# A graph transformer on one core: the last tile's query asked for earlier, and the order of two layer norms in eight blocks

## The chip, the cores and the metric

The kernel runs on one core of a Trainium2 chip. A core has five engines, each with its own queue of instructions that it works through in order: TensorE (PE in the profile; its weight loads are PEld) for matrix products and transposes, VectorE (DVE), ScalarE (ACT), GpSimd (POOL) and SyncE (SP), which only issues transfers. Engines wait for each other by semaphores. The metric is the device time of a whole execution in microseconds, of which 1.7 us lie outside the span from the first to the last instruction in the profiled execution.

## The reference, cut to what matters

Two layers of a transformer on a graph of 2708 nodes with 512 features and 8 heads; a node attends only to its neighbours and itself.

```python
mask = adj.astype(jnp.float32) + jnp.eye(n, dtype=jnp.float32)
q = (h @ Wq.T + bq).reshape(n, N_HEADS, D_K)       # k, v alike
scores = jnp.einsum('nhd,mhd->hnm', q, k) / jnp.sqrt(jnp.float32(D_K))
scores = jnp.where(mask[None, :, :] == 0, -1e9, scores)
ctx = jnp.einsum('hnm,mhd->nhd', jax.nn.softmax(scores, axis=-1), v)
h1 = _layer_norm(h + ctx.reshape(n, 512) @ Wo.T + bo, ln1_g, ln1_b)
ff = jax.nn.relu(h1 @ W1.T + b1) @ W2.T + b2       # 512 -> 2048 -> 512
h2 = _layer_norm(h1 + ff, ln2_g, ln2_b)
```

All values are float32. `_layer_norm` subtracts the mean of a row, multiplies by (variance + eps) to the power of -0.5 and by a gain, and adds a shift. The adjacency matrix is sparse: some nine neighbours a node.

## The kernel before, in words

The function `by_edges` computes attention along the edges. Nodes are sorted by the length of their neighbour lists and cut into 22 tiles of 128 nodes (tile 21 has 20). `CAPS` holds the longest list of each tile, from 22 entries in tile 0 down to 3 in tile 21. A tile's list is worked in chunks of two neighbours (`chunks_of`, L1133): tile 0 has eleven chunks, tile 16 four, tile 21 two.

**Attention (`attend`, L1750).** The tiles come in the order of `blocks` (L1745), pairs of tiles: (20, 19), (18, 17), (8, 9), (7, 10) and so on, ending with (1, 16), (21, 0). For a chunk, `loads` (L1240) has GpSimd gather the rows of keys and values (`gather`, L1112, one indirect transfer per neighbour; L1113 in the profile), three chunks ahead (`EARLY`) into five buffers (`KVB`). VectorE multiplies keys by the query (L1150) and sums over each head (L1156). One step later ScalarE takes the exponentials (L1169) and multiplies the second neighbour's values by them (L1176), VectorE multiplies the first neighbour's (L1182) and adds to the sum (L1189). Two and three steps later `sums` and `divided` finish the tile (L1197 to L1220).

A tile's query `q` is fetched by `asked` (L1122) into one of three buffers (`QB`). In layer 0 the fetch is a gather on GpSimd's queue, in layer 1 a plain transfer on SP's. `attend` asks for the next tile's query right behind the first chunk of a tile (L1778). GpSimd's queue thus holds key gathers, queries, residual rows, scatters and the small powers of the layer norms in one order.

**Feed-forward.** The tiles are taken by the pairs of `blocks`, k = 0 to 10. In layer 0, blocks k = 2 to 9 use `feed_forward_by_seven` (L1605), which computes the second product of a pair in a 2x2 scheme with seven products in place of eight. Sixteen steps f of it produce `pf` (L1645, TensorE), `ft` (L1656, the ReLU on ScalarE), sums of pairs of `ft` on VectorE (`sums`, L1617 to L1620) and the seven products (`products`, L1635). `pf` has two places in PSUM, so a `pf` waits until the `ft` of the one before last is evicted. At the end VectorE puts the pieces together (L1688 to L1695) and norms the two tiles one after the other.

**The layer norm (`norm`, L1265)** is a chain: statistics (L1269, VectorE), their aggregate (L1271), variance plus eps (L1273), the power of -0.5 on GpSimd (`rd`, L1275), and meanwhile on VectorE the first scaling (L1276: minus mean, times gain), and then the second (L1279: times `rd`, plus shift), which waits for `rd`.

**Around it.** The loop at L1917 interleaves by hand: between the steps f of a block it runs `advance`, which takes steps of `attend` from a budget of costs (`PACE7`), the next block's output projection (`attended`, L1426) at f = 10 to 12, and at f = 5 to 8 the keys and values of the next layer (`keys_values`, L1700) for the block before. The latter begins with the transposes of both normed tiles on TensorE (`flip`, L1281; L1285 in the profile). The order of the instructions on each engine is the order in which the program writes them.

## Time and profile before

| | |
|---|---|
| median of three runs | 1836.17 us (1834.93 to 1837.08) |
| the profiled execution | 1835.82 us, of which span 1834.1 us |
| PE, DVE, ACT, POOL busy | 1809.1, 1458.5, 948.7, 798.9 us |
| granted TensorE clock | 0.997 of full speed |
| moved by DMA | 393.80 MB, 215 GB/s |
| layer norms | 88 |
| query gathers on GpSimd in layer 0 | 19, 1.04 us each to issue |

A row of the costliest groups reads: line, engine, operation, output<-inputs, shapes and count; busy us in total and mean ns of one; and the idle time of the engine just before these instructions with what ended it. A row of a timeline reads: start us, length us, engine, line, operation; in brackets the idle time of the engine before it and what ended that. Ends of matmuls are modelled, so distances between starts are safer than lengths.

### The profile page before, as it was taken

How to read it: one execution, taken by the hardware profiler on the slowest of the kernel's cores; microseconds unless marked ns; L12 is line 12 of the kernel's file. 1: busy time of each engine (PE TensorE's matmuls, PEld its weight loads, DVE VectorE, ACT ScalarE, POOL GpSimd, SP SyncE). 2: the span in 40 equal slices, each digit the busy share in tenths (PEclk: the TensorE clock that was granted, in tenths of full speed). 3: DMA queues.
4: the chain of work that ended last, by engine and by line, in shares of the span. 5: the costliest groups of instructions: out<-in, count | busy, mean ns of one | idle time of the engine just before them, and what ended most of it. 6: DMA issues, size and time to landing. Idle time of an engine off the chain costs nothing.

```text
span 1834.1 us, 22527 instructions
## 1 busy us (share of the span) xinstructions
PE 1809.1 (99%) x6563; PEld 1163.0 (63%) x6563; DVE 1458.5 (80%) x2447; ACT 948.7 (52%) x3271; POOL 798.9 (44%) x745
## 2 busy tenths in 40 slices
PE   9999999999999999999999999999999999999998
PEld 4444456666677867778677644666666666666666
DVE  5987778988989889898795247887898898889853
ACT  5770435644556545564553113655665665567531
POOL 3234755534455544454440032443554554456302
PEclk9999999999999999999999999999999999999999
DMA  9987987756576575665652776845564664555300
GB/s 342 376 324 255 376 277 246 235 173 230 201 253 228 193 235 194 220 234 179 219 194 69 261 254 256 303 143 196 178 213 160 218 235 159 203 196 191 132 17 21
DMA packets 158061, 393.80 MB, mean 215 GB/s; under 512 B 17514, under 2 KB 60894, under 8 KB 157928
## 3 DMA queue, kind: packets, MB, share of 16 engines
q0 software_dynamic: 70608, 252.12, 39.9%
q1 hardware_dynamic: 77162, 118.55, 18.7%
q10 hardware_dynamic: 10158, 21.61, 3.1%
q8 instruction: 53, 0.87, 0.2%
q14 instruction: 80, 0.66, 0.1%
HBM read 338.78 MB, written 53.44 MB: 214 GB/s over the span
## 4 chain that ended last, share of the span: by engine, by line
PE 81%; DVE 10%; ACT 3%; issue 3%; DMA 2%; POOL 1%; POOLq 0%; DVEq 0%; ACTq 0%
PE pf L1515 17%; PE a L1488 16%; PE q L620 8%; PE o L620 8%; PE pf L1645 7%; PE k L620 7%; PE v L620 7%; PE c L1635 4%; PE a L1635 3%; PE tp L1285 2%; DVE sc L1156 2%; DVE kv L1150 2%; ACT kv L1176 1%; POOL rd L1275 1%; DVE acc L1189 1%
## 5 line engine op out<-in xcount | busy, mean ns | idle before, releaser
L1113 POOL DMA_INDIRECT kv<-kv_d,listed x420 | 523.5, 1246 | 294.5 <-DVE acc L1189 133.3
L1515 PE MATMUL pf<-hT,w 128*128 128x256 f32 (+1 forms) x1792 | 393.2, 367 | 0.2 <-ACT ft L1526 0.2
L1515 PEld LDWEIGHTS pf<-hT,w 128*128 128x128 f32 x1792 | 323.5, 190 | 103.3 <-issue 64.4
L1488 PE MATMUL a<-w,ft 128*128 128x512 f32 x800 | 373.1, 592 | 0.0
L1176 ACT ACTIVATE kv<-kv,p 128x64 f32<-128x64 f32 x1232 | 311.0, 335 | 5.0
L1275 POOL TENSOR_TENSOR rd<-va,mhalf 128x1 f32<-128x1 f32 (+1 forms) x88 | 80.1, 910 | 525.4 <-DVE va L1273 525.3
L1150 DVE TENSOR_TENSOR kv<-kv,q 128x1024 f32<-128x1024 f32 (+1 forms) x222 | 257.0, 1157 | 19.6 <-DMA q<-q_d,ident_i 16.5
L1156 DVE TENSOR_REDUCE sc<-kv 128x16 f32<-128x1024 f32 (+1 forms) x222 | 257.9, 1162 | 7.6
L1645 PE MATMUL pf<-hT,w 128*128 128x256 f32 x1024 | 233.2, 379 | 3.8 <-ACT ft L1656 3.8
L1189 DVE TENSOR_TENSOR acc<-acc,kv 128x1024 f32<-128x1024 f32 (+2 forms) x178 | 205.4, 1154 | 35.9 <-ACT kv L1176 21.0
L1488 PEld LDWEIGHTS a<-w,ft 128*128 128x128 f32 x800 | 150.2, 190 | 113.2 <-issue 101.3
L1645 PEld LDWEIGHTS pf<-hT,w 128*128 128x128 f32 x1024 | 193.9, 190 | 37.8 <-issue 7.9
L1526 ACT ACTIVATE ft<-pf,b 128x256 f32<-128x256 f32 (+1 forms) x208 | 94.8, 458 | 197.8 <-PE pf L1515 197.6
L1169 ACT ACTIVATE p<-sc,listed 128x8 f32<-128x8 f32 x420 | 104.0, 296 | 157.2 <-DVE sc L1156 145.4
L620 PE MATMUL o<-wo,cT 128*128 128x512 f32 x336 | 151.0, 593 | 1.0 <-ACT cT L1290 1.0
L1656 ACT ACTIVATE ft<-pf,b 128x256 f32<-128x256 f32 x96 | 44.8, 467 | 160.4 <-PE pf L1645 160.4
L1182 DVE TENSOR_TENSOR kv<-kv,p 128x512 f32<-128x512 f32 (+1 forms) x178 | 123.4, 693 | 4.0 <-ACT p L1169 4.0
L620 PEld LDWEIGHTS o<-wo,cT 128*128 128x128 f32 x336 | 63.5, 190 | 74.7 <-issue 65.5
L745 DVE MAX8 tops<-code 128x8 f32<-128x247 f32 (+2 forms) x242 | 78.8, 400 | 28.8 <-ACT code L740 28.8
L1279 DVE SCALAR_TENSOR_TENSOR h<-h,rd,ln_b 128x512 f32<-128x512 f32 (+1 forms) x88 | 66.1, 751 | 44.2 <-POOL rd L1275 44.2
L1220 ACT ACTIVATE cx<-acc,su 128x64 f32<-128x64 f32 (+1 forms) x352 | 88.2, 333 | 12.9 <-DVE su L1212 7.4
L1447 DVE TENSOR_TENSOR h<-o,xb 128x512 f32<-128x512 f32 (+1 forms) x44 | 30.3, 688 | 79.2 <-PE o L620 66.3
(231 smaller groups left out, 2325.7 us busy)
## 6 DMA issues: line engine op xcount, KB each, us to landing
aj<-in_adj SPq DMA_DIRECT2D x42, 677.0 KB, 7.0
forms<-form_d SPq DMA_DIRECT2D x168, 128.0 KB, 4.5
kv_d<-kvs ACTq DMA_DIRECT2D x21, 512.0 KB, 6.7
xg<-in_xT SPq DMA_DIRECT2D x19, 512.0 KB, 7.6
w<-in_W SPq DMA_DIRECT2D x16, 512.0 KB, 6.2
kv<-kv_d,listed POOLq DMA_INDIRECT x420, 6.2
zT_d<-zT SPq DMA_DIRECT2D x22, 256.0 KB, 5.2
xb_d<-h SPq DMA_DIRECT2D x21, 256.0 KB, 6.2
```

The source lines that it names most:

```text
L620: nc.tensor.matmul(o[:r], xs(c), wm[:, c, :], start=(c == 0), stop=(c == NC - 1))
L1113: return nc.gpsimd.indirect_dma_start(out=to, out_offset=None, in_=table[:, :], in_offset=bass.IndirectOffsetOnAxis(ap=s, axis=0), bounds_ ...
L1150: nc.vector.tensor_tensor(kv[:r, :c, :DM], kv[:r, :c, :DM], self.q[:r].unsqueeze(1).to_broadcast([r, c, DM]), ALU.mult,)
L1156: nc.vector.tensor_reduce(self.sc[:r, s0 : s0 + c, :], kv[:r, :c, :DM].rearrange("p s (h d) -> p s h d", d=DK), AX.X, ALU.add,)
L1169: nc.scalar.activation(p[:r, s, :], self.sc[:r, s, :], AF.Exp, bias=minus[:r, g, s : s + 1])
L1176: nc.scalar.activation(to[:, i, hd], kv[:r, i, DM + h * DK : DM + (h + 1) * DK], AF.Copy, scale=p[:r, s0 + i, h : h + 1],)
L1182: nc.vector.tensor_tensor(to[:, 0, :].rearrange("p (h d) -> p h d", d=DK), kv[:r, 0, DM:].rearrange("p (h d) -> p h d", d=DK), p[:r, s0, : ...
L1189: nc.vector.tensor_tensor(self.acc[:r, :c, :], self.acc[:r, :c, :], kv[:r, :c, DM:], ALU.add)
L1488: nc.tensor.matmul(a[:r, cols], fts[f][:, c0 : c0 + r], self.w2[f // 2][:, f % 2, cols], start=(f == 0), stop=(f == NFC - 1),)
L1515: nc.tensor.matmul(pf[:, :w], self.w1[f // 2][:, c, f % 2 * P : f % 2 * P + P], hT[:, c, :w], start=(c == 0), stop=(c == NC - 1),)
L1635: nc.tensor.matmul(to, left, right, start=start, stop=stop)
L1645: nc.tensor.matmul(pf[:, :W], self.w1[j][:, c, f % 2 * P : f % 2 * P + P], hT[:, c, :], start=(c == 0), stop=(c == NC - 1),)
```

## The change

`norm` takes a function that it calls between its two scalings. In `feed_forward_by_seven` the first tile's `norm` is given one that issues the second tile's statistics (`spread`); the second tile's `norm` then gets these and issues none. VectorE's order becomes: first scaling of the first tile, statistics of the second, second scaling of the first, and then the second tile from its aggregate on. This is in eight blocks of layer 0.

In `attend` the query of the last tile (tile 0) is asked for in the third chunk of the third tile from the end (tile 16), while tile 16's query and tile 21's are still held; the third buffer is that of tile 1. Before, it was asked for behind the first chunk of tile 21, two chunks later. This is in both layers. On GpSimd's queue in layer 0 the query's gather moves ahead of four key gathers; SP's order stays the same. The counts of instructions are unchanged.

```diff
-    def norm(z, r, gain, shift, st=None):
+    def norm(z, r, gain, shift, st=None, between=None):
...
             z[:r], z[:r], mv[:r, 0:1], gain[:r], ALU.subtract, ALU.mult
         )
+        if between:
+            between()
         nc.vector.scalar_tensor_tensor(z[:r], z[:r], rd[:r], shift[:r], ALU.mult, ALU.add)
+
+    def spread(z):
+
+        st = small.tile([P, 6], F32, tag="st", name="st")
+        nc.vector.bn_stats(st, z)
+        return st
...
-            for z in hs:
-                norm(z, P, self.g2, self.e2)
+            stB = []
+            norm(zA, P, self.g2, self.e2, between=lambda: stB.append(spread(zB)))
+            norm(zB, P, self.g2, self.e2, stB[0])
             yield list(hs)
...
-        q = asked(n, order[0])
+        q, later = asked(n, order[0]), None
...
                 if q is None and g != order[-1]:
-                    q = asked(n, order[order.index(g) + 1])
+                    q, later = later or asked(n, order[order.index(g) + 1]), None
+                if g == order[-3] and i == 2:
+                    later = asked(n, order[-1])
```

## The prediction

> **What bounds the kernel now.** I read the page first, then the waits of TensorE alone, then the timelines of the engines around each of those waits, and last the granted clock by stretches.

> ```profile
> PE 1809.1 (99%) x6563; PEld 1163.0 (63%) x6563; DVE 1458.5 (80%) x2447; ACT 948.7 (52%) x3271; POOL 798.9 (44%) x745
> ...
> L1279 DVE SCALAR_TENSOR_TENSOR h<-h,rd,ln_b 128x512 f32<-128x512 f32 (+1 forms) x88 | 66.1, 751 | 44.2 <-POOL rd L1275 44.2
> ```

> TensorE has work in 99% of the span, so a stall of another engine is worth only the part that reaches TensorE. The 44.2 us that VectorE idles for `rd` are such stalls: 0.50 us each, 88 times. The waits of TensorE (us in total, times, longest) show what reaches it:

> ```profile
> PE tp L1285 <- DVE h L1279: 5.2, 8, 1.6
> PE pf L1645 <- ACT ft L1656: 3.8, 3, 2.2
> ```

> The first is a tile's transposes waiting for the second scaling of a layer norm; the second holds one wait of 2.24 us. The change touches both. TensorE's timeline prints all eight places of the first: five are behind a block of seven products. The widest, behind k=2, on VectorE, on GpSimd, and then on TensorE (start us, length us; in brackets the idle time before):

> ```profile
> 478.60 0.74 DVE L1276 SCALAR_TENSOR_TENSOR h<-h,mv,ln_g 128x512 f32<-128x512 f32 x1
> 479.80 0.75 DVE L1279 SCALAR_TENSOR_TENSOR h<-h,rd,ln_b 128x512 f32<-128x512 f32 x1 [0.45 <-POOL rd L1275]
> 480.46 0.69 DVE L1269 BATCH_NORM_STATS2 st<-h 128x6 f32<-128x512 f32 x1
> 481.19 0.18 DVE L1271 BATCH_NORM_AGGREGATE mv<-st 128x2 f32<-128x6 f32 x1
> ...
> 482.66 0.75 DVE L1279 SCALAR_TENSOR_TENSOR h<-h,rd,ln_b 128x512 f32<-128x512 f32 x1 [0.44 <-POOL rd L1275]
> ```
> ```profile
> 478.84 0.93 POOL L1275 TENSOR_TENSOR rd<-va,mhalf 128x1 f32<-128x1 f32 x1 [7.24 <-DVE va L1273]
> ```
> ```profile
> 481.21 0.60 PE L1285 MATMUL tp<-ident,h 128*128 128x128 f32 x4
> 483.46 0.66 PE L1285 MATMUL tp<-ident,h 128*128 128x128 f32 x4 [1.65 <-DVE h L1279]
> ```

> VectorE stands still for `rd` of the pair's first tile (A), then does the second tile (B) from its statistics on; A's transposes find A ready, B's wait until B's last scaling ends.

> **Part 1: statistics of B between A's scalings.** No instruction is added or removed; in eight blocks (k=2 to 9) one 0.69 us instruction moves up by one place. From the rows of k=2: an instruction behind a scaling starts 0.66 us after it (479.80 to 480.46), so B's statistics start at 479.26. A full-width instruction of 0.68 us that nobody waits for is followed after 0.60 us (L1692 to L1693, 476.07 to 476.67), so A's second scaling starts at 479.86, 0.06 later than now; `rd` landed at 479.77. B's aggregate follows at 479.86 + 0.66 = 480.52 instead of 481.19. B is ready **0.67 us** earlier. This is more than the idle 0.45, since the aggregate no longer waits for the end of the statistics just before it. Bounds: 0.45 (the idle alone) and 0.73. A's 0.06 costs nothing: A ends at 480.6, its transposes start at 481.21; the other blocks leave A 1.9 us and more. GpSimd's two `rd` follow each other in its queue with nothing between them, and the key gather behind them comes 0.67 earlier.

> TensorE gains the smaller of 0.67 and its own wait. That wait is the distance between the starts of A's and B's transposes less 0.43, which four transposes take (905.49 to the next start, 905.92): k=2, 2.25 - 0.43 = 1.82; k=4 and k=5, 0.89 - 0.43 = 0.46 each; k=6, 0.04; k=7, 1.01 - 0.43 = 0.58; k=8, 1.04 - 0.43 = 0.61; k=3 and k=9, none. So 0.67 + 0.46 + 0.46 + 0.04 + 0.58 + 0.61 = **2.8 us** (2.3 with 0.45, 2.9 with 0.73). Where TensorE's gain is only its own wait, VectorE gains as much or more, so it does not become late somewhere else.

> A rule that speaks against this: `rd` takes 0.93 beside a scaling, but 0.58 where no VectorE instruction runs (at 448.32 and 913.18). [...] A scaling has two tensor inputs, the statistics one. Today VectorE idles exactly while `rd` makes up what the scaling cost it; afterwards statistics run there. If they held `rd` for their 0.69 as a scaling does, A's second scaling would slip to about 480.5 and the 0.67 be gone: 2.4 us in sum instead of 5.2. No row has statistics over an `rd`. The nearest: 51 key gathers that run beside a one-input reduction (L1156) alone take 0.95 to 1.04 us, those beside no VectorE instruction 0.99; beside a scaling some 1.5. I take `rd` as unchanged.

> **Part 2: the last tile's query.** In layer 0 its gather goes to GpSimd's queue in tile 16's third chunk instead of behind tile 21's first: past four key gathers, those of tile 0's first two chunks. GpSimd, then VectorE and TensorE:

> ```profile
> 871.69 0.96 POOL L1113 DMA_INDIRECT kv<-kv_d,listed  x1 [0.30 <-issue]
> 882.33 1.75 POOL L1113 DMA_INDIRECT kv<-kv_d,listed  x1 [9.68 <-DVE acc L1189]
> 884.38 1.51 POOL L1113 DMA_INDIRECT kv<-kv_d,listed  x1 [0.30 <-issue]
> ...
> 889.40 1.00 POOL L1113 DMA_INDIRECT q<-q_d,ident_i  x1 [0.30 <-issue]
> ```
> ```profile
> 894.76 1.22 DVE L1150 TENSOR_TENSOR kv<-kv,q 128x1024 f32<-128x1024 f32 x1 [5.41 <-DMA q<-q_d,ident_i]
> ```
> ```profile
> 897.38 0.60 PE L1285 MATMUL tp<-ident,cx 128*128 128x128 f32 x4
> 900.22 1.99 PE L1645 MATMUL pf<-hT,w 128*128 128x256 f32 x8 [2.24 <-ACT ft L1656]
> ```

> The query is asked at 889.40, lands at 894.6, and VectorE waits 5.41 us. ScalarE evicts `ft` (899.72) only behind the exponentials and products of that chunk, and TensorE's next `pf` waits for the place of that `ft`: 900.22 - 897.38 - 0.43 = **2.4 us**. In its new place the gather follows the one at 871.69 and starts at about 873, inside GpSimd's 9.68 us of idleness, so the four it passes lose nothing (and the two behind its old place start 1.3 us sooner). Its buffer, one of three, is tile 1's, last read before tile 16 began, some 20 us earlier; it waits for nothing. What is late next: the keys of the same chunk, asked at 882.33 and 884.38 because their buffer comes free only then. The trace gives 5.2 and 5.8 us to landing for these two, so 890.2. VectorE then starts at 890.2 instead of 894.76, 4.5 us sooner, `ft` is evicted at about 895.6, and TensorE asks for its place at 897.8: 2.2 us to spare. All 2.4 go. Bounds: 0 (keys landing after 894.6) and 2.4. Behind it, products and projections of k=8 are fed by a VectorE that is 3.5 to 4.5 us ahead of today, so TensorE does not run into it.

> In layer 1 the query comes by SP, whose order of instructions is the same in both kernels, and no L1150 there waits for a query: nothing.

> **The clock.** The one stall of the same size that stays is at 978 to 980.84 (start to end; span, then PE, PEld, DVE, ACT, POOL busy, PEclk, DMA):

> ```profile
> 979.00:980.00 1.00, 0.00 (x0) 0.00 (x0) 0.48 (x2) 1.00 (x6) 0.00 (x0) 1.00 0.00 0
> ...
> 982.00:983.00 1.00, 1.00 (x5) 0.00 (x0) 0.00 (x0) 0.00 (x0) 0.00 (x0) 0.50 0.07 16
> ```

> It runs back through VectorE and ScalarE to TensorE's own `v` at 964.95, so it moves along with TensorE and stays 2.7 us long. Behind it the clock is 0.50 for 3.3 us, which costs about 1.7; behind the 2.4 us at 898 to 900.2 it stayed at 1.00. [...]

> **Sum.** 2.8 + 2.4 = 5.2 us. The profiled execution has 1834.1 us of span and 1835.82 in all; it becomes 1828.9 and 1830.6. The median of the runs, 1836.17, lies 0.35 higher: **1831.0**.

> **Rivals.** (a) Only one part pays: statistics hold `rd` (1836.17 - 2.4 = 1833.8), or the keys land late (1836.17 - 2.8 = 1833.4). For it: no row of statistics beside `rd`, and landing times move with DMA load. Against it: the reductions beside gathers, and 2.2 us to spare. (b) The clock falls otherwise: 1829.3 or 1832.7. (c) Slower, by one mechanism: `rd` of A comes behind a key gather in GpSimd's queue, as at 913.79, where a scaling waited 1.50 us for an `rd` behind two gathers. Now B's statistics are done, but B's aggregate stands behind the waiting scaling. `rd` 1.5 us late puts A's second scaling at 481.3, B's aggregate at 481.97, 0.78 later than today: six blocks lose 4.7, less part 2's 2.4 is 2.3 slower, 1838.5. It is slower than before from 0.4 us per block on, and by over 0.2% from 1.0 on (`rd` 1.7 late; the longest gather took 2.0: 1841). Against it: GpSimd has been idle for 4.4 us or more before each of these eight `rd`. (d) The change does nothing that TensorE feels: 1836.2.

> **How the numbers follow.** Both parts 0.62 (own range 1830 to 1832.4), (a) 0.20, (b) 0.10, (c) 0.06, (d) 0.02. About 0.2%, 3.7 us, is what a measurement can tell from no change: faster means below 1832.5. That is nearly all of the first case and the better half of (b) and a little of (a): 0.71; (c) is over 1839.8 in about half its cases, with some room for what I do not see: 0.05; the rest, 0.24. The range leaves out (c), (d) and the best of (b): 1829.2 to 1834.0.

> **What would show it.** Right: in the eight blocks the wait of A's second scaling for `rd` is gone or under 0.1; B's transposes wait only behind k=2, some 1.1 us; no L1150 waits for a query at tile 0, it waits 1 us or less for keys; `pf` at about 898 has no wait. Wrong: `rd` over 1.1 us beside statistics; a new wait of TensorE between 890 and 1070; a second stretch of half clock; a stall at 980 longer than 2.7.

## The result, and the profile after

The changed kernel takes **1829.87 us** (median of seven runs, 1827.33 to 1831.03) where the kernel before takes 1836.17 (seven runs, 1834.38 to 1837.08). The ratio is 0.9962, with a 95% interval of 0.9953 to 0.9971: 7.0 us less (0.0038 x 1836.17), between 5.3 and 8.6. The profiled execution took 1828.87 us with a span of 1827.1, 7.0 less than the 1834.1 of before.

First the page's row for the second scaling, then that line's idle time by releaser (us, times), then the waits of TensorE (us in total, times, longest), all of the changed kernel:

```profile
L1281 DVE SCALAR_TENSOR_TENSOR h<-h,rd,ln_b 128x512 f32<-128x512 f32 (+1 forms) x88 | 65.9, 749 | 39.5 <-POOL rd L1275 39.5
...
  POOL rd L1275: 39.5, 80
```
```profile
PE tp L1293 <- DVE h L1281: 3.1, 4, 1.0
PE o L615 <- ACT cT L1298: 2.4, 1, 2.4
...
PE pf L1653 <- ACT ft L1664: 1.6, 2, 0.8
...
PE c L1643 <- DMA forms<-form_d: 0.4, 1, 0.4
```

Of 88 waits for `rd`, 80 are left: eight are gone, one in each of the eight blocks. TensorE's waits for transposes go from 5.2 us in eight places to 3.1 in four, and its wait for `ft` from 3.8 to 1.6: the one of 2.24 us is missing.

The pair of k=2, by the timelines of VectorE, GpSimd and TensorE (start, length, and in brackets the idle time before):

```profile
478.09 0.74 DVE L1276 SCALAR_TENSOR_TENSOR h<-h,mv,ln_g 128x512 f32<-128x512 f32 x1
478.75 0.69 DVE L1286 BATCH_NORM_STATS2 st<-h 128x6 f32<-128x512 f32 x1
479.36 0.73 DVE L1281 SCALAR_TENSOR_TENSOR h<-h,rd,ln_b 128x512 f32<-128x512 f32 x1
480.01 0.17 DVE L1271 BATCH_NORM_AGGREGATE mv<-st 128x2 f32<-128x6 f32 x1
...
481.47 0.75 DVE L1281 SCALAR_TENSOR_TENSOR h<-h,rd,ln_b 128x512 f32<-128x512 f32 x1 [0.44 <-POOL rd L1275]
```
```profile
478.33 0.93 POOL L1275 TENSOR_TENSOR rd<-va,mhalf 128x1 f32<-128x1 f32 x1 [7.24 <-DVE va L1273]
```
```profile
480.69 0.60 PE L1293 MATMUL tp<-ident,h 128*128 128x128 f32 x4
482.27 0.66 PE L1293 MATMUL tp<-ident,h 128*128 128x128 f32 x4 [0.98 <-DVE h L1281]
```

From A's first scaling to B's last one it is now 3.38 us (478.09 to 481.47), before 4.06 (478.60 to 482.66): 0.68 less. `rd` still takes 0.93 with the statistics beside it. TensorE's wait falls from 1.65 to 0.98.

The query of tile 0, by GpSimd, VectorE and TensorE:

```profile
870.37 1.03 POOL L1113 DMA_INDIRECT q<-q_d,ident_i  x1 [0.30 <-issue]
879.79 1.73 POOL L1113 DMA_INDIRECT kv<-kv_d,listed  x1 [8.39 <-DVE acc L1189]
```
```profile
887.13 1.24 DVE L1150 TENSOR_TENSOR kv<-kv,q 128x1024 f32<-128x1024 f32 x1 [0.26 <-DMA kv<-kv_d,listed]
```
```profile
894.85 0.60 PE L1293 MATMUL tp<-ident,cx 128*128 128x128 f32 x4
895.29 1.89 PE L1653 MATMUL pf<-hT,w 128*128 128x256 f32 x8
```

The gather lies in what was GpSimd's idle time; VectorE waits 0.26 us for keys instead of 5.41 for the query; `pf` follows the transposes at once.

**Where 7.0 us came from in these two executions.** Following the starts of the same instructions on TensorE through both traces, the layer norms of the eight blocks give 3.0, the query 2.5, and 1.6 comes at the gap behind tile 21's transposes. That gap is as long as it was (2.40 us idle at 975.14), but before the clock fell to half behind it, and here it does not; in a single execution that is chance (see "Where a gap falls" below). The start of the kernel and waits for the slots read from `form_d`, which come and go between executions (0 to 2.1 us in the profiles shown here), net to nearly nothing. So the waits give 5.5, against the forecast's 5.2, and the clock gives the rest.

### The profile page after: what moved, and what is told of

The parts are those of the page before. It is cut to its first block, busy times and chain, and to the rows that moved or that the text cites. A ratio compares the mean times of both kernels' runs of the same rounds, so it can differ in the third digit from the quotient of the medians.

```text
span 1827.1 us, 22528 instructions
## 1 busy us (share of the span) xinstructions
PE 1807.5 (99%) x6563; PEld 1162.6 (64%) x6563; DVE 1457.5 (80%) x2447; ACT 949.1 (52%) x3271; POOL 798.9 (44%) x745
## 4 chain that ended last, share of the span: by engine, by line
PE 89%; DVE 5%; issue 2%; ACT 2%; DMA 1%; POOL 1%; POOLq 0%; SPq 0%; DVEq 0%
PE pf L1523 18%; PE a L1496 17%; PE pf L1653 9%; PE k L620 8%; PE v L620 8%; PE q L620 8%; PE o L620 8%; PE c L1643 4%; PE a L1643 3%; PE tp L1293 2%; DVE sc L1156 1%; DVE kv L1150 1%; DMA forms<-form_d 1%; PE a L1677 1%; PE a L1673 1%
## 5 line engine op out<-in xcount | busy, mean ns | idle before, releaser
L1113 POOL DMA_INDIRECT kv<-kv_d,listed x420 | 524.0, 1248 | 291.2 <-DVE acc L1189 133.9
L1275 POOL TENSOR_TENSOR rd<-va,mhalf 128x1 f32<-128x1 f32 (+1 forms) x88 | 80.5, 914 | 520.6 <-DVE va L1273 520.5
L1150 DVE TENSOR_TENSOR kv<-kv,q 128x1024 f32<-128x1024 f32 (+1 forms) x222 | 256.9, 1157 | 13.3 <-DMA q<-q_d,ident_i 10.9
L1156 DVE TENSOR_REDUCE sc<-kv 128x16 f32<-128x1024 f32 (+1 forms) x222 | 257.9, 1162 | 7.6
L1189 DVE TENSOR_TENSOR acc<-acc,kv 128x1024 f32<-128x1024 f32 (+2 forms) x178 | 205.4, 1154 | 37.6 <-ACT kv L1176 23.0
```

What stands on the lines that cost most here:

```text
L1113: return nc.gpsimd.indirect_dma_start(out=to, out_offset=None, in_=table[:, :], in_offset=bass.IndirectOffsetOnAxis(ap=s, axis=0), bounds_ ...
L1150: nc.vector.tensor_tensor(kv[:r, :c, :DM], kv[:r, :c, :DM], self.q[:r].unsqueeze(1).to_broadcast([r, c, DM]), ALU.mult,)
L1156: nc.vector.tensor_reduce(self.sc[:r, s0 : s0 + c, :], kv[:r, :c, :DM].rearrange("p s (h d) -> p s h d", d=DK), AX.X, ALU.add,)
L1189: nc.vector.tensor_tensor(self.acc[:r, :c, :], self.acc[:r, :c, :], kv[:r, :c, DM:], ALU.add)
```

## The experiments

The question was what part of the gain beyond 5.2 us belongs to the two gaps of TensorE (at 898, which the change closes, and at 975, which stays) through the clock. Two readings stood against each other: that only the waits count and the clock is chance of either sign, and that each of the two gaps halves the clock behind it in many executions, so that closing one saves more than its length. A stretch of half clock lasts 3.41 us in the traces (in the kernel before from 981.46 to 984.88). It costs half of that, 1.7 us, and takes 0.0009 off an execution's mean granted clock (1.7 of 1830). The clock is listed in thousandths, so a single execution cannot always be told apart; means over executions can. They are rough all the same: behind TensorE's last product every profiled execution has a stretch of half clock up to its end, 3.5 to 6.7 us of it (6.1 in the kernel before, 3.5 in the changed kernel), which costs no time and takes another 0.0010 to 0.0018 off the mean. In the texts of the expectations, "the kernel before" of each group is the one run on the same chip with it.

### Each part alone, both, and both with the gap filled

e1_norms: part 1 alone.

```diff
-                if g == order[-3] and i == 2:
-                    later = asked(n, order[-1])
```

> Only the order of the two layer norms is changed; the query stays where it was. If the sum of the waits of TensorE is right, 2.8 us less than before (2.3 to 3.2), and the wait of TensorE for ft at about 898 stays at 2.2 to 2.4 us. If statistics of the second tile held the power of -0.5 on GpSimd, 0.3 us or less. If the gain beyond 5.2 us that the changed kernel shows comes from the clock of TensorE at the gap at 898, none of it is here, since the gap is: not over 3.2.

e2_query: part 2 alone.

```diff
-            stB = []
-            norm(zA, P, self.g2, self.e2, between=lambda: stB.append(spread(zB)))
-            norm(zB, P, self.g2, self.e2, stB[0])
+            for z in hs:
+                norm(z, P, self.g2, self.e2)
```

> Only the query is asked for sooner; the norms are as before. By the waits alone 2.4 us less than before (2.2 to 2.6) and the five waits for the second tile's scaling as before. By the clock, that is, if the gap of 2.4 us at 898 drops the clock in some executions, 2.4 plus up to 1.7 by its share: 2.7 to 4.0. If keys land late and take over the wait, under 1.

e3_both: the changed kernel again, with no edit.

> The changed kernel again, on the same chip as the two halves. By the waits alone 5.2 us less than before, and the sum of the two halves. By the clock 5.5 to 7, and still the sum of the two halves, with what goes beyond 5.2 in the half that moves the query.

e4_fill: the changed kernel, with three idle products in the gap at 975. They write into the place of the projection's result, which the projection then overwrites.

```diff
-    def project(xs, r, wm, name, other=False):
+    def project(xs, r, wm, name, other=False, fill=0):
...
+        for i in range(fill):
+            cols = slice(0, DM if i else DM // 2)
+            nc.tensor.matmul(o[:, cols], ones, wm[:, 0, cols], start=True, stop=True)
...
-                o = project(lambda c: cT[:, c, :r], r, self.wo, "o")
+                fill = 3 if self.n == 0 and r <= Q4 else 0
+                o = project(lambda c: cT[:, c, :r], r, self.wo, "o", fill=fill)
```

> The changed kernel with three idle products (2.15 us, ones times Wo into the bank that the next product overwrites) in front of the projection of tile 21, in the gap of 2.4 to 2.7 us at 975 in which TensorE waits for the eviction of cT. Output as before. By the waits alone the same time as the changed kernel within 0.3 us, or 0.2 slower where the products reach past the gap. By the clock there is no gap left that can drop it: no stretch of half clock before the end in the profile, and 0.3 to 1.7 us less than the changed kernel, by the share of executions in which the clock fell at 975.

Measured on one chip:

| | median us | mean us (runs) | ratio to before, 95% | mean granted clock |
|---|---|---|---|---|
| before | 1835.84 | 1835.93 (26) | | 0.9970 |
| e1_norms | 1833.73 | 1833.64 (11) | 0.9988 (0.9979 to 0.9997) | 0.9969 |
| e2_query | 1832.11 | 1832.05 (11) | 0.9976 (0.9967 to 0.9985) | 0.9975 |
| e3_both | 1830.76 | 1830.04 (10) | 0.9970 (0.9960 to 0.9979) | 0.9976 |
| e4_fill | 1828.49 | 1828.44 (5) | 0.9960 (0.9946 to 0.9973) | 0.9984 |

By the means, part 1 alone gives 2.3 us, part 2 alone 3.9, both 5.9. The parts add up. Part 1 by itself leaves the clock where it was (0.9970 to 0.9969); part 2 raises it by 0.0005.

The profile of e1_norms shows why. TensorE's timeline around the gap at 898, which part 1 alone leaves open, and the stretches around it (bounds, span, then PE, PEld, DVE, ACT, POOL busy, the granted clock, DMA share and GB/s):

```profile
894.15 0.60 PE L1293 MATMUL tp<-ident,cx 128*128 128x128 f32 x4
897.14 3.23 PE L1653 MATMUL pf<-hT,w 128*128 128x256 f32 x8 [2.39 <-ACT ft L1664]
900.17 1.06 PE L620 MATMUL o<-wo,cT 128*128 128x512 f32 x1
```
```profile
894.33:897.74 3.41, 1.02 (x7) 0.73 (x6) 3.24 (x7) 3.38 (x14) 1.71 (x2) 1.00 0.21 51
897.74:901.15 3.41, 3.41 (x9) 2.36 (x8) 3.31 (x10) 2.78 (x12) 2.80 (x3) 0.50 0.84 215
```

The clock falls to 0.50 behind the 2.39 us gap, and the eight `pf` take 3.03 us to the next start (897.14 to 900.17) where the changed kernel takes 1.73 (895.29 to 897.02). The changed kernel has no gap there; at 975 it has, and e3's execution shows the half clock at that one:

```profile
971.09:974.50 3.41, 1.32 (x8) 0.47 (x8) 0.73 (x3) 2.89 (x13) 0.00 (x0) 1.00 0.00 0
974.50:977.92 3.42, 3.42 (x12) 2.77 (x11) 2.97 (x5) 1.14 (x4) 0.00 (x0) 0.50 0.07 20
```

e4 only adds work. TensorE's timeline there, in the gap:

```profile
971.42 2.31 PE L615 MATMUL o<-wo,ones 128*128 128x256 f32 x6
973.99 1.53 PE L618 MATMUL o<-wo,cT 128*20 128x512 f32 x8 [0.26 <-ACT cT L1301]
```

The projection starts no sooner, and yet the mean is 1.6 us lower than e3's and the mean clock 0.0008 higher. (The expectation had 2.15 us of products; the timeline has 2.31.) That speaks for the clock as a cost of the gaps, though with ten and five runs the 1.6 is uncertain by 1.8 either way (standard deviations of 1.8 and 1.4); later runs return to it.

### Is the query late again, is `rd` held, and what closes the gap at 975

e5_later: the query asked one chunk later, behind the key gathers of tile 0's first chunk.

```diff
-                if g == order[-3] and i == 2:
+                if g == order[-3] and i == 3:
```

> The changed kernel with the query asked one chunk later, in tile 16's fourth chunk, so behind the two key gathers of tile 0's first chunk and ahead of those of its second. If the working of the prediction holds, the query lands some 1.3 us behind the keys, VectorE waits for it by about that much longer, and TensorE's pf at about 895 still has no wait: the time of the changed kernel within 0.6 us. If there is nothing to spare, 1.3 us slower than the changed kernel.

e6_two: the last addition into B, which reads two tensors from SBUF, moved between A's scalings as well, ahead of the statistics.

```diff
-            nc.vector.tensor_tensor(pair(zB), pair(zB), twice(u34[:, L]), ALU.add)
             stB = []
-            norm(zA, P, self.g2, self.e2, between=lambda: stB.append(spread(zB)))
+            def beside():
+                nc.vector.tensor_tensor(pair(zB), pair(zB), twice(u34[:, L]), ALU.add)
+                stB.append(spread(zB))
+            norm(zA, P, self.g2, self.e2, between=beside)
```

> The changed kernel in which the addition that makes the second tile whole (L1703, two inputs in SBUF) also moves between the first tile's scalings, in front of the second tile's statistics. If an instruction with two inputs in SBUF holds the power of -0.5 on GpSimd, and one with a single input does not, the power of the first tile, 0.93 us beside the scaling alone, takes 1.5 us here or the addition starts late; the second scaling comes behind the statistics in any case, so the time is that of the changed kernel within 0.4 us. If nothing but the scaling itself matters, it stays at 0.93.

e7_hold: in block k=9 the attention's step behind f = 9, which is the division of tile 0's sums, is left for later, so that on ScalarE it comes behind the eviction of tile 21's `cT`.

```diff
-                advance((PACE7 if seven else (PACE if k else PACES)[n])[f])
+                if not (seven and k == NB - 2 and f == 9):
+                    advance((PACE7 if seven else (PACE if k else PACES)[n])[f])
```

> The changed kernel with one step of the attention held back in block k=9: what advance would do at f = 9 is done at f = 10, so on ScalarE the division of tile 0 comes behind the eviction of cT of tile 21 in place of ahead of it. By the waits the projection of tile 21 has no wait any more (it had 2.4 us at 975), and the transposes of tile 0's context wait some 0.9 instead: 1.7 us less than the changed kernel. By the clock, no gap of over 2 us is left in the middle of the kernel, and 1.2 to 1.7 more are gained: 2.9 to 3.4 less in sum, and no half clock before the end.

e8_before_fill: the kernel before, with the idle products of e4.

> The kernel before with the three idle products in front of the projection of tile 21, so that of the two long gaps of TensorE only the one at 898 is left. Output as before. By the clock it gains on the kernel before what the products gain on the changed kernel (1.4 to 1.6 us), and it loses to the changed kernel with the products by 5.2 plus the clock's share of the gap at 898 (0.6 of 1.7 us, by the mean clocks of the runs): 5.8 to 6.5. By the waits alone it is as slow as the kernel before, and 5.2 behind the changed one with the products.

| | median us | mean us (runs) | ratio to before, 95% | mean granted clock |
|---|---|---|---|---|
| before | 1836.69 | 1836.82 (15) | | 0.9967 |
| e5_later | 1829.35 | 1828.87 (5) | 0.9958 (0.9945 to 0.9972) | 0.9978 |
| e6_two | 1829.39 | 1829.64 (5) | 0.9963 (0.9950 to 0.9977) | 0.9974 |
| e7_hold | 1827.02 | 1827.54 (5) | 0.9952 (0.9939 to 0.9966) | 0.9980 |
| e8_before_fill | 1834.58 | 1834.94 (11) | 0.9992 (0.9982 to 1.0001) | 0.9983 |

**e5.** VectorE waits 1.83 us for the query, which is asked at 884.31, and TensorE feels nothing of it:

```profile
889.30 1.23 DVE L1150 TENSOR_TENSOR kv<-kv,q 128x1024 f32<-128x1024 f32 x1 [1.83 <-DMA q<-q_d,ident_i]
```
```profile
895.50 0.60 PE L1293 MATMUL tp<-ident,cx 128*128 128x128 f32 x4
895.94 1.89 PE L1653 MATMUL pf<-hT,w 128*128 128x256 f32 x8
```

So there is slack in the forecast's "2.2 us to spare": a query over 1.5 us later than the keys costs nothing measurable.

**e6.** VectorE, then GpSimd, at k=2:

```profile
476.49 0.74 DVE L1276 SCALAR_TENSOR_TENSOR h<-h,mv,ln_g 128x512 f32<-128x512 f32 x1
477.14 0.68 DVE L1706 TENSOR_TENSOR h<-h,u 128x512 f32<-128x512 f32 x1
477.86 0.69 DVE L1286 BATCH_NORM_STATS2 st<-h 128x6 f32<-128x512 f32 x1
478.47 0.73 DVE L1281 SCALAR_TENSOR_TENSOR h<-h,rd,ln_b 128x512 f32<-128x512 f32 x1
```
```profile
476.72 0.93 POOL L1275 TENSOR_TENSOR rd<-va,mhalf 128x1 f32<-128x1 f32 x1 [6.76 <-DVE va L1273]
```

`rd` takes 0.93 with an addition of two tensors behind the scaling, as it does with statistics there and with nothing there. A second hold of `rd`, for which e6 was made, does not show: whatever the scaling costs `rd` (0.93 against 0.58 alone), the instruction behind the scaling adds nothing. The total is the changed kernel's within the interval.

**e7.** It lies 9.3 us under the kernel before, where the changed kernel lies 5.9 and 7.5 under it in the groups that have it: 1.8 to 3.4 more, with 2.9 to 3.4 expected. The projection no longer waits; TensorE's timeline:

```profile
973.48 1.05 PE L615 MATMUL o<-wo,cT 128*20 128x512 f32 x8
974.47 1.30 PE L1293 MATMUL tp<-ident,cx 128*128 128x128 f32 x4
975.60 0.60 PE L1643 MATMUL a<-forms,ft 128*128 128x256 f32 x2
```

The 2.40 us of waiting are gone and some 0.7 come back at the transposes behind it (974.47 to 975.60 where four take 0.43). No execution of the five has a clock below 0.998.

**e8.** Without either part of the change, the idle products take 1.9 us off the mean (1836.82 to 1834.94), with an interval that just reaches no change, and raise the mean clock by 0.0016. Its executions lie at 0.998 and 0.999, so they show little of a loss at 898, where the gap is still open; the profiled one has none (2.54 us of gap, and the clock stays at 1.00 behind it). That left the share of the gap at 898 uncertain.

### The gap at 898 by itself, and the fastest version again

e9_both is the changed kernel, e10_hold repeats e7, e12_fill repeats e4, and e11_norms_fill is part 1 alone with the idle products of e4, so that the gap at 898 is the only long one left:

```diff
-                if g == order[-3] and i == 2:
-                    later = asked(n, order[-1])
...
+        for i in range(fill):
+            cols = slice(0, DM if i else DM // 2)
+            nc.tensor.matmul(o[:, cols], ones, wm[:, 0, cols], start=True, stop=True)
...
+                fill = 3 if self.n == 0 and r <= Q4 else 0
```

> The changed kernel once more, as the base for the next three on the same chip. Both readings: 5.5 to 7 us under the kernel before (means). The gap of 2.7 us at 975 is there, so some executions should have a granted clock of 0.997 (one stretch of half clock) and the others 0.998 or 0.999; no execution should be at 0.996, since that takes two stretches and only one gap of over 2 us is left.

> The changed kernel with the attention's advance at step f = 9 of block k = 9 left out, once more. The wait of the last tile's first projection for cT is gone, so 2.4 us of waiting less 0.7 us that come back before the transposes, and no half clock there. If the gain is a gain of waits and clock: 1.7 us from the wait in every execution and up to 1.7 from the clock in some, so 2 to 3 us under the changed kernel of this call, and all executions at a granted clock of 0.998 or 0.999. If the earlier 1.3 us (means of two different chips' bases) was chance: within 0.8 us of the changed kernel.

> Part 1 alone, with the three idle products in the gap at 975, so that the gap at 898 is the only one of over 2 us. If the gap at 898 by itself drops the clock in a good part of the executions: granted clock 0.997 in these and 0.998 or 0.999 in the others, and this kernel 3.2 to 4.2 us above the changed kernel with the same idle products (2.5 of wait, and 1.7 times that part). If the gap at 898 does not drop the clock by itself: all executions at 0.998 or 0.999, and the distance is the wait alone, 2.2 to 2.7 us.

> The changed kernel with the three idle products in the gap at 975. No gap of over 2 us is left in this part: all executions at a granted clock of 0.998 or 0.999. Against the changed kernel of this call it should be under it by 1.7 us times the share of that kernel's executions that lose the clock at 975: 0.5 to 1.5 us; if the earlier 1.6 us was chance, no difference or a loss of 0.1 to 0.3 us.

| | median us | mean us (runs) | ratio to before, 95% | mean granted clock |
|---|---|---|---|---|
| before | 1836.96 | 1837.05 (15) | | 0.9967 |
| e9_both | 1829.59 | 1829.56 (5) | 0.9960 (0.9945 to 0.9976) | 0.9974 |
| e10_hold | 1824.79 | 1825.66 (5) | 0.9938 (0.9923 to 0.9953) | 0.9990 |
| e11_norms_fill | 1833.26 | 1833.51 (11) | 0.9980 (0.9971 to 0.9989) | 0.9982 |
| e12_fill | 1829.36 | 1829.40 (5) | 0.9959 (0.9944 to 0.9974) | 0.9986 |

**e11.** TensorE's timeline and the stretches around 898:

```profile
894.96 0.60 PE L1296 MATMUL tp<-ident,cx 128*128 128x128 f32 x4
898.13 2.57 PE L1657 MATMUL pf<-hT,w 128*128 128x256 f32 x8 [2.58 <-ACT ft L1668]
```
```profile
898.00:900.00 2.00, 1.87 (x7) 1.64 (x8) 1.97 (x3) 1.46 (x6) 1.69 (x2) 0.85 0.74 203
900.00:902.00 2.00, 2.00 (x4) 1.01 (x3) 1.93 (x8) 1.91 (x8) 1.69 (x2) 0.50 0.74 207
902.00:904.00 2.00, 2.00 (x5) 0.91 (x4) 1.86 (x5) 2.00 (x10) 1.39 (x3) 0.79 0.99 389
```

A gap of 2.58 us, alone, halves the clock behind it. e11 lies 4.1 us above e12, which differs from it by part 2 only; the wait is 2.5 of that. By clock, 0.0004 lies between them, half a stretch for each execution or 0.8 us; the 0.8 that remains is within what the scatter of 11 and 5 runs leaves open (about 1.6 either way, from standard deviations of 1.7 and 1.3). The expectation looked for the drop in executions at 0.997; the profiled one has the drop and is listed at 0.998, since its half clock at the end is short (3.7 us). So a single listed clock does not tell whether this gap dropped it.

**e9 and e12.** The changed kernel has executions at 0.997 and 0.998 and none at 0.996, as expected with one gap left. But e12 is only 0.2 us under it, where e4 was 1.6 under e3, although the mean clock rises by 0.0012. The second comparison by itself shows no gain in time, but its 0.2 is uncertain by 1.8 either way. Weighted by their scatter, the three comparisons with and without idle products (1.6, 1.9, 0.2) give 1.3, with some 0.9 either way.

**e10.** The fastest version again: 3.9 us under e9 by the means (highest e10 1827.82, lowest e9 1828.12), all five executions at 0.999. Expected were 2 to 3; 1.7 of waiting and 1.7 of clock make 3.4.

```profile
972.70 1.06 PE L615 MATMUL o<-wo,cT 128*20 128x512 f32 x8
...
974.66 0.33 PE L1293 MATMUL tp<-ident,cx 128*128 128x128 f32 x1 [0.15 <-ACT cx L1220]
974.83 0.60 PE L1643 MATMUL a<-forms,ft 128*128 128x256 f32 x2
```

In its profiled execution the transposes behind the projection cost about 0.7 as in e7 (973.68 to 974.83, less 0.43). Its ratio of 0.9938 (0.9923 to 0.9953) beats both kernels of this case.

```profile
896.12:899.54 3.42, 1.86 (x11) 1.42 (x9) 3.25 (x7) 2.24 (x10) 0.74 (x1) 1.00 0.47 162
899.54:902.95 3.41, 2.73 (x11) 2.04 (x12) 3.38 (x5) 2.78 (x12) 2.80 (x3) 1.00 0.65 166
...
978.05:981.46 3.41, 1.00 (x8) 0.47 (x8) 1.36 (x7) 3.21 (x14) 0.00 (x0) 1.00 0.00 0
981.46:984.88 3.42, 3.42 (x14) 1.65 (x8) 1.65 (x3) 0.85 (x4) 0.00 (x0) 0.50 0.02 5
```
```profile
970.24:973.65 3.41, 2.50 (x14) 1.76 (x12) 3.17 (x11) 1.10 (x5) 0.00 (x0) 1.00 0.00 0
973.65:977.07 3.42, 1.93 (x12) 0.94 (x13) 0.60 (x2) 2.30 (x10) 0.00 (x0) 1.00 0.02 5
977.07:980.48 3.41, 3.41 (x18) 3.02 (x17) 3.24 (x6) 1.14 (x4) 0.00 (x0) 1.00 0.38 115
...
1816.74:1820.15 3.41, 1.50 (x7) 0.97 (x6) 1.77 (x5) 0.00 (x0) 0.40 (x1) 1.00 0.03 5
1820.15:1823.57 3.42, 0.00 (x0) 0.00 (x0) 0.86 (x2) 0.00 (x0) 1.59 (x2) 1.00 0.07 25
```

TensorE's idle time in a window is its length less the first of the busy times. Before, the gap at 898 is split between two windows, 1.56 and 0.68 us, and the clock stays; the gap at 978 lies whole in one, 2.41 us, and the next window runs at 0.50. In the changed kernel the same gap is split, 0.91 and 1.49, and the clock stays; at its end a window with 1.92 us idle (the row is rounded) is still followed by one at 1.00. e1's two gaps lie whole in a window each (2.39 and 2.41), and both drop the clock; of e3's, 2.09 us lie in one, and it drops. From the first rise to the end of the work, this holds for every window of the 14 traces: with 2.09 us idle (e3) or more the next one runs at half clock, with 1.92 (the changed kernel) or less it does not (by modelled ends of products).

An estimate from these figures, with the limit put at 2.0 us: a gap of 2.4 us escapes when a bound cuts it in the middle 1.6 us (twice 2.0 less 2.4). If all positions are alike, that is 1.6 of 3.41, and the gap drops the clock in 0.53 of the executions, for 0.53 x 1.7 = 0.9 us on average.

## Why the prediction was right or wrong

The forecast, 1831.0 within 1829.2 to 1834.0, was too high by 1.1 us against the median; by the ratio the gain was 7.0 where 5.2 was forecast, just at the low end of the range (1836.17 - 7.0 = 1829.2). The direction, the two mechanisms and their places hold; the size was off by a term of the sum.

**Part 1, B ready 0.67 sooner.** Measured 0.68 at k=2. A's scaling no longer waits in any of the eight blocks, and TensorE waits only at k=2, 0.98 (forecast 1.1). TensorE's shifts sum to 3.0 in the two traces, forecast 2.8 (2.3 to 2.9). In time, part 1 alone gave 2.3 (0.6 to 3.9 by its interval), and 2.0 on top of part 2 (e2 to e3): no contradiction to 2.8, but no sharper than that.

**Part 1, what spoke against it.** `rd` was taken as unchanged beside statistics, and it is: 0.93. e6 goes further: an addition of two tensors behind the scaling does not make it longer either (0.93 at 476.72). The rows show a longer `rd` with the scaling (0.93, against 0.58 where no VectorE instruction runs) and nothing from the next instruction; whether `rd` had read its inputs by then, no run here shows. Rival (a) of held `rd` and rival (c), `rd` behind a key gather, did not occur: no scaling of A waits.

**Part 2, the wait.** The query goes out at 870.37, the keys land and VectorE starts at 887.1; forecast were 873 and 890.2 on a timeline that now runs 2.5 to 3 us earlier at this place. 2.4 were forecast for TensorE, 2.5 were found. The cover of 2.2 us was real (e5). In layer 1 TensorE gains nothing, as forecast: its lead over the kernel before is 7.3 us at 985 and 7.0 at the end.

**The clock: the step that failed.** The sum is 2.8 + 2.4, with nothing for the clock; its 1.7 us stand beside the sum, with either sign, as rival (b): 1829.3 or 1832.7. The clock's term measured about 0.9 us. That a gap of this size can halve the clock the forecast had from the row at 982 (0.50), but it used that row for one gap only. One execution with 1.00 behind the gap at 898 was taken as that gap's price, and the clock as a coin with two sides. It is not for the gap that goes: removing it cannot make its half clock more frequent. (It does move the gap behind it against the windows, and that part has both signs.) Nor do the two gaps of the profile before differ as 2.4 and 2.7 us: TensorE idles 2.24 in the one and 2.40 in the other, and what parted them was the position. e1's profile and e11's show the clock at 0.50 behind exactly that gap.

Four comparisons with and without part 2 put the mean clock 0.0004 (before to e2), 0.0007 (e1 to e3), 0.0006 (before to e3) and 0.0004 (e11 to e12) higher, about half a stretch per execution, some 0.9 us. Each of the four is uncertain by about its own size, and they share runs; but the windows give the same 0.9 by another way (0.53 x 1.7). So part 2 was worth 2.5 plus about 0.9 where 2.4 was put down; by time it is 3.9 (before to e2), 3.6 (e1 to e3) and 4.1 (e11 to e12). The mean of these, 3.9, leaves 0.5 that waits and clock do not account for, and that the scatter allows. With 2.8 + 2.4 + 0.9 the forecast would have been 1830.1, 0.2 from the median: between the first case and the better half of rival (b), which the forecast held apart. The gain would have been 6.1 us, inside the interval of 5.3 to 8.6.

**The gap that stays.** "It moves along with TensorE and stays 2.7 us long" is right but for the length, which by idle time is 2.40 before and after. The forecast named a second stretch of half clock as a sign of error; there was none, and even the first is missing in the profiled execution, where the gap is split, while others have it (e3, e9). That the profile before had this drop and not the one at 898, and the profile after had none, is luck of the position.

**What stays open.** How often each gap drops the clock is known from means and from the estimate above only. The idle products raised the mean clock of the changed kernel (twice) and of the kernel before, by 0.0008 to 0.0016; the time followed fully in e4, in part in e8 and hardly in e12, and whether that is more than scatter, no run here shows. In e8 the clock rose by nearly two stretches, though only one gap was filled. Filling the gap at 898 was not tried. The same kernel lay 9.3 us under before in e7 and 11.4 in e10, at mean clocks of 0.9980 and 0.9990; in their profiled executions that difference of the clock lies behind TensorE's last product, where it costs nothing:

```profile
1818.65:1825.29 6.64, 0.00 (x0) 0.00 (x0) 0.75 (x1) 0.00 (x0) 1.40 (x2) 0.50 0.12 44
```
```profile
1820.43:1824.74 4.31, 0.00 (x0) 0.00 (x0) 0.00 (x0) 0.00 (x0) 0.16 (x1) 0.50 0.17 65
```

## What to carry to other kernels

Where TensorE is busy for 99% of the span, price a stall by its own length and by what its clock does afterwards (here 2.4 us, and 1.7 more where the clock fell); one profiled execution tells only one outcome of the second (behind the gap of 2.40 us the changed kernel's stayed at 1.00, behind that of 2.41 e9's fell to 0.50), so the chance of it belongs in the sum as a one-sided gain when the stall goes. The trace can give that chance: find the bounds at which the clock changes (here 3.41 us apart), and see how much of the stall one window can hold. To shorten a chain over two engines, put an independent instruction of the next tile where the first waits for its partner, and count every instruction behind it: here the gain was larger than the idle time that was filled (0.68 us against 0.45). Look for the next stall of the same size before finishing: leaving one step of the attention for later was worth another 3.9 us on the same chip (e10 against e9).

## What had not been expected of the hardware

- A pause of TensorE of 2.4 to 2.6 us (2.39 in e1, 2.58 in e11) was enough for 3.41 us at a granted clock of 0.50 behind it (e1: eight `pf` in 3.03 us instead of 1.73), in some executions of a program and not in others. In the 14 traces it was so whenever 2.09 us or more of idle time lay in one window of 3.41 us, and never with 1.92 or less.
- Work that nobody needs seems to have paid: with three idle products in a pause, 2.31 us of them, the mean time was lower by 1.6 us (e4), 1.9 (e8) and 0.2 (e12), though the projection behind them started no sooner. Each by itself is hardly clear of the scatter; together they are (1.3, some 0.9 either way).
- `rd` on GpSimd took 0.58 us with no VectorE instruction beside it (448.32 and 913.18 of the kernel before) and 0.93 beside a scaling, whether nothing (478.84 of the kernel before), statistics (478.33 of the changed kernel) or an addition of two tensors (476.72 of e6) followed the scaling.
